# Cross-attention with layer norm on one core: the scores of two tiles in one TensorE visit

## The chip, the cores and the metric

The kernel runs on one core of one Trainium2 chip. Its time is the device time of one execution in microseconds (us), the median of several runs. The engines are TensorE (PE; its weight loads are shown apart as PEld), VectorE (DVE), ScalarE (ACT), GpSimd (POOL) and SyncE (SP), which issues most DMAs. Each engine works through its own instructions in the order in which the kernel's text names them; semaphores make one wait for another.

## The reference

Four batches of 2048 query rows (512 wide) attend to 77 context rows each, with 16 heads of 32. A mask of 77 bytes a row is non-zero where a key is left out. Behind the output projection stand a residual and a layer norm with gamma and beta.

```python
qs = (q @ wq).reshape(Bq, Lq, H, HD).transpose(0, 2, 1, 3)
ks_ = (k @ wk).reshape(Bq, Lk, H, HD).transpose(0, 2, 1, 3)
vs = (v @ wv).reshape(Bq, Lk, H, HD).transpose(0, 2, 1, 3)
scores = jnp.einsum('bhqd,bhkd->bhqk', qs, ks_) / jnp.sqrt(jnp.float32(HD))
scores = jnp.where(mask[:, None, :, :], -jnp.inf, scores)
attn = jnp.einsum('bhqk,bhkd->bhqd', jax.nn.softmax(scores, axis=-1), vs)
out = attn.transpose(0, 2, 1, 3).reshape(Bq, Lq, H * HD) @ wo + q
mu = jnp.mean(out, axis=-1, keepdims=True)
var = jnp.mean((out - mu) ** 2, axis=-1, keepdims=True)
return (out - mu) / jnp.sqrt(var + EPS) * gamma + beta
```

A row whose keys are all masked gives NaN in the reference.

## The kernel before

The 8192 query rows are 64 tiles of 128; two tiles are a pair (`u` and `u + 1`, pair number n = u / 2), four a group, sixteen a batch. The wide products (queries, output) keep full precision by splitting each operand into a high and a low part and adding three matmuls, so that a visit to the query projection (`q_visit`, L177) or the output projection (`o_proj`, L517) is 12 matmuls of 512 columns. A tile passes through these steps:

- `scores` (L309): 32 small matmuls, which the trace shows as 64. Head h = 4g + j has its 32 rows of queries and keys in row group j of the array; a tile's rows are dealt to two halves of columns. Each row group j has a PSUM bank of its own for its four heads (g = 0 to 3), 77 columns each: four banks a tile.
- `maxima` (L324), one DVE instruction a head: the score plus the mask's bias, negated, into `pbuf`, and the least of them as the exponential's bias.
- `exps` (L339), one ACT instruction a head, with the sum of its row; `recip` on DVE; `normalise` (L350), one POOL instruction a tile.
- `transp` (L373), a DVE transposition in 32x32 blocks into `B`; `regroup` (L385), twelve DMAs a pair that SP issues, put the blocks into `PT`.
- `av` (L419), 16 small matmuls a pair (32 in the trace); `av_hi` (ACT, L468) and `av_lo` (DVE, L472) empty its two banks into a high and a low part.
- `o_proj`, `residual` (DVE, L520), `moments` (DVE, L525 and L530, then four short POOL instructions, L534 to L537), `scale` (ACT, L543), `affine` (two POOL instructions, L547 and L548) and `store`.

Next to this the transposed x of a later group is loaded (`load_xT`), its high part made by ACT (`cast_xT`, L166), its low part by POOL (`split_xT`, L170), and the queries of later tiles are projected and copied from PSUM by DVE (`q_evac`, L194).

PSUM has eight banks, dealt out in a ring (`bank`): a new one waits for the readers of the one handed out eight before. `pbuf` has three buffers, the tile numbers modulo 3.

The mask of a batch is loaded in the pair of tile 10 of the batch before (`load_mask`), becomes a bias of 0 or -3.0e38 in the pair of tile 12 (`mask_bias`, L286 and L287), and `mask_min` (L291) and `mask_nan` (L295, L296) of the pair of tile 14 make a column `nz` that is EPS, or NaN where all keys of a row are masked. It is added to the variance, so that NaN comes out.

The order is written by hand: L714 to L831 is a loop over the pairs of tiles 0 to 53, and for the last ten tiles `ORDER` names each step by a letter, a tile and a part, which `do` carries out. In a pair of the loop TensorE's order is scores(u), o_proj(u-6), q_visit, av(n-2), scores(u+1), o_proj(u-5), q_visit.

Of the kernel before, what the change touches and what calls it, by code (L numbers as in the profile page):

```python
# [20 lines left out]
HD = 32  # L21
NK = 77
TAIL_K = 19
NK2 = NK + TAIL_K
NP = H // 2
PW = 160
GH = 4
NG = H // GH
# [40 lines left out]
def xattn_layernorm(  # L69
# [15 lines left out]
    nc = tc.nc  # L85
    NB = mask.shape[0]
    TPB = mask.shape[2]
# [8 lines left out]
    ring, kept, rows, summed = [], set(), {}, set()  # L96

    def bank(name):
# [25 lines left out]
    unit = ident.bitcast(F32R)  # L124
    mhalf, mneg, gates = small[:, 0:2], small[:, 2:4], small[:, 4:5]
    last_st = small[:, 8:20].rearrange("p (n s) -> p n s", n=2)
# [24 lines left out]
    def keys_of(h):  # L151
        return slice(TAIL_K, NK2) if h % 2 == 0 else slice(0, NK)
# [124 lines left out]
    def load_mask(b):  # L277
        m8 = sb.tile([P, TPB, NK], U8, tag="m8", bufs=1, name=f"m8_{b}")
        nc.sync.dma_start(m8, mask[b])
        mb = sb.tile([P, TPB, NK2], BF16, tag="mb", name=f"mb_{b}")  # L280
        nz = sb.tile([P, TPB], F32, tag="nz", name=f"nz_{b}")
        bat[b] = (mb, nz, m8)

    def mask_bias(b, ts=slice(0, TPB)):
        mb, nz, m8 = bat[b]
        nc.vector.tensor_scalar(mb[:, ts, TAIL_K:], m8[:, ts], MASKED, None, ALU.mult)  # L286
        nc.vector.tensor_scalar(mb[:, ts, :TAIL_K], m8[:, ts, NK - TAIL_K :], MASKED, None, ALU.mult)  # L287

    def mask_min(b):
        mb, nz, m8 = bat[b]  # L290
        nc.vector.tensor_reduce(nz, m8, AX.X, ALU.min)  # L291

    def mask_nan(b):
        nz = bat[b][1]
        nc.vector.tensor_scalar(nz, nz, 3.0e38, 10.0, ALU.mult, ALU.mult)  # L295
        nc.vector.tensor_scalar(nz, nz, 0.0, EPS, ALU.mult, ALU.add)  # L296


    def scores(t):
        qs = qd[t // 4]  # L300
        nmax[t] = sb.tile([P, H], F32, tag="nm", bufs=3, name=f"nm_{t}")
        sums[t] = sb.tile([P, H], F32, tag="sum", bufs=3, name=f"sum_{t}")
        sc = scs[t] = [bank(f"sc_{t}_{j}") for j in range(GH)]
        for g in range(NG):
            for half in range(0, P, P // 2):
                for j in range(GH):
                    q = slice(HD * j, HD * (j + 1))
                    r0 = (t % 4) * P + half
                    nc.tensor.matmul(  # L309
                        sc[j][half : half + P // 2, g * NK : (g + 1) * NK],  # L310
                        qs[q, g, r0 : r0 + P // 2],
                        kct[q, g, t // TPB, keys_of(j)],
                        start=True,
                        stop=True,
                    )

    def maxima(t, lo, hi):
        pb = pbuf[t % NPB]
        mb = bat[t // TPB][0]
        nm = nmax[t]  # L320
        for h in HEADS[lo:hi]:
            g, j = divmod(h, GH)
            i = slot(h)
            nc.vector.tensor_tensor_reduce(  # L324
                pb[:, i // 2, (i % 2) * NK : (i % 2 + 1) * NK],
                scs[t][j][:, g * NK : (g + 1) * NK],
                mb[:, t % TPB, keys_of(h)],
                -1.0,
                3.0e38,
                ALU.add,  # L330
                ALU.min,
                accum_out=nm[:, i : i + 1],
            )
# [53 lines left out]
    def regroup(b):  # L387
        for n in range(12):
            regroup_part(b, n, nc.sync)
# [132 lines left out]
    def moments(t):  # L522
        b, tt = divmod(t, 2)
        st = sb.tile([P, 6], F32, tag="st", bufs=3, name=f"st_{t}")
        nc.vector.bn_stats(st, od[t])  # L525
# [4 lines left out]
        nc.vector.bn_aggr(mv[:, tt, :], st)  # L530
        nz = bat[t // TPB][1]
        if tt == 1:
            k = (t - 1) % TPB
# [54 lines left out]
    def rsqrt_one(t):  # L588
        mv = mvs[t, 1]
        k = t % TPB  # L590
        eps = bat[t // TPB][1][:, k : k + 1]
        if t in summed:
            nc.gpsimd.tensor_scalar(mv[:, 2:3], mv[:, 1:2], 1.0 / D, eps, ALU.mult, ALU.add)
        else:
            nc.gpsimd.tensor_tensor(mv[:, 2:3], mv[:, 1:2], eps, ALU.add)
        nc.gpsimd.tensor_tensor(mv[:, 2:3], mv[:, 2:3], mhalf[:, :1], ALU.pow)
# [35 lines left out]
    nc.gpsimd.memset(mhalf, -0.5)  # L632
    nc.gpsimd.memset(mneg, -1.0)
    for pb in pbuf:
        nc.gpsimd.memset(pb[:, :, 2 * NK :], 0.0)
# [57 lines left out]
    for m in range(0, NG, 2):  # L693
        keys_evac(pks, m)
    mask_min(0)
    for c in range(0, NC_D, 2):
# [16 lines left out]
    evac = [(0, 0)]  # L713
    for u in range(0, 2 * CUT, 2):  # L714
        n = u // 2
# [79 lines left out]
        if u == 0:  # L795
            mask_nan(0)
            split_wv()
            recip(0)
# [37 lines left out]
        "+": residual, "u": rsqrt_one, "y": centre, "z": finish, "k": scale, "f": affine, "w": store,  # L836
        "v": bias_one, "K": stretch, "G": shift, "p": pool_scale, "I": act_mean, "J": act_squares, "M": keep,
    }
# [5 lines left out]
    def do(op, k, part=0, queue="s"):  # L844
# [8 lines left out]
        elif op in tile_parts:  # L853
            tile_parts[op](k, q4 * part, q4 * part + q4)
        elif op == "s":
# [23 lines left out]

    for word in ORDER.split():  # L880
        op, (k, part) = word[0], (word[1:] + ".").split(".")[:2]
        queue = part[-1:] if part[-1:].isalpha() else ""
        do(op, int(k), int(part[: len(part) - len(queue)] or 0), queue or "s")

# [47 lines left out]
```

## Time and profile before

| What | us |
|---|---|
| Median of three runs (514.13 to 518.13) | 514.41 |
| Profiled execution: its span, from the first to the last instruction | 510.7 |
| Median less that span | 3.7 |
| PE busy in the span | 502.1 |
| PEld busy | 387.3 |
| DVE busy | 472.1 |
| ACT busy | 471.2 |
| POOL busy | 424.3 |

The profiled execution is one other than the timed ones; of it the span is known, and the runs' time counts what lies around the span too. A row of the page's groups reads: line, engine, operation, what it writes and from what, shapes and count, then busy time and the mean of one, then idle time before it and what ended it. A row of the timeline reads: start, time to the end of the last of the rows merged into it, engine, line, operation, shapes, count. A row of stretches reads: from and to, length, then the busy time of PE, PEld, DVE, ACT and POOL with the count of instructions, the granted TensorE clock as a share of full speed, the busy share of the DMA engines, and GB/s. Times of matmuls overlap, so two starts tell more than a duration.

### The profile page before, as it was taken

What the parts mean: (1) busy time and instruction counts of PE and PEld (TensorE: products, weight loads), DVE (VectorE), ACT (ScalarE), POOL (GpSimd) and SP (SyncE); (2) the same over time, 40 slices, a digit from 0 to 9 for tenths busy, and PEclk for the clock granted to TensorE, in tenths of its full rate; (3) what the DMA queues carried; (4) which work ended last, traced back from release to release, by engine and by line L of the source; (5) the groups of instructions that cost most, each with busy time, mean ns of one, the idle gap of its engine ahead of it and who ended that gap; (6) DMA issues with size and microseconds to landing.
All of it is one profiled execution on the core that took longest, in us unless ns stands there. A gap on an engine that the chain in (4) does not pass through costs nothing.

```text
span 510.7 us, 20467 instructions
## 1 busy us (share of the span) xinstructions
PE 502.1 (98%) x6864; PEld 387.3 (76%) x6864; DVE 472.1 (92%) x2574; ACT 471.2 (92%) x2239; POOL 424.3 (83%) x382
## 2 busy tenths in 40 slices
PE   8999999999999999999999999999999999999994
PEld 6987777777777777777777777777777777777784
DVE  6798999899999888989999898889999989999997
ACT  6798999999899999999899999999899999999861
POOL 0659359988799988888989998898889989999894
PEclk9999999999999999999999999999999999999998
DMA  8946867888777888789777897788887778767665
GB/s 304 400 155 150 224 177 197 217 237 221 189 207 201 233 215 224 193 222 246 185 202 218 228 230 192 181 235 230 223 217 192 211 198 234 192 185 216 166 207 207
DMA packets 58280, 109.34 MB, mean 214 GB/s; under 512 B 9203, under 2 KB 10739, under 8 KB 58176
## 3 DMA queue, kind: packets, MB, share of 16 engines
q1 hardware_dynamic: 55776, 103.19, 73.1%
q0 software_dynamic: 1872, 4.20, 2.9%
q8 instruction: 55, 0.90, 0.8%
q10 hardware_dynamic: 528, 0.66, 0.4%
q14 instruction: 49, 0.40, 0.3%
HBM read 41.53 MB, written 16.78 MB: 114 GB/s over the span
## 4 chain that ended last, share of the span: by engine, by line
PE 87%; DVE 5%; DMA 4%; SPq 2%; POOL 1%; issue 1%; ACT 1%; DVEq 0%; POOLq 0%
PE pq L177 30%; PE po L517 29%; PE pa L419 10%; PE sc L309 10%; PE sc L517 3%; DMA PT<-B 2%; DVE B L373 2%; PE pv L243 2%; PE pk L203 1%; SPq L385 1%; DVE pbuf L324 1%; DMA stage_a<-wq 1%; PE pq L669 1%; POOL pbuf L350 0%; DVE q L194 0%
## 5 line engine op out<-in xcount | busy, mean ns | idle before, releaser
L339 ACT ACTIVATE pbuf<-pbuf,nm 128x77 f32<-128x77 f32 x1024 | 352.5, 350 | 15.0 <-DVE nm L324 13.6
L339 ACT ACTIVATION_READ_ACCUMULATOR pbuf<-pbuf,nm 128x1 f32 x1024 | 195.3, 191 | 0.0
L324 DVE CUSTOM_DVE_ANT_0 pbuf<-sc,mb 128x77 f32<-128x77 f32 x1020 | 169.9, 230 | 21.8 <-PE sc L309 21.5
L350 POOL TENSOR_TENSOR pbuf<-pbuf,ri 128x1232 f32<-128x1232 f32 x63 | 142.2, 2258 | 17.8 <-DVE ri L345 11.0
L177 PE MATMUL pq<-xth,wqh 128*128 128x512 f32 (+1 forms) x256 | 98.8, 386 | 0.0
L177 PE MATMUL pq<-xtl,wqh 128*128 128x512 f32 (+1 forms) x256 | 98.0, 383 | 0.0
L177 PE MATMUL pq<-xth,wql 128*128 128x512 f32 (+1 forms) x256 | 97.9, 383 | 0.0
L373 DVE STREAM_TRANSPOSE B<-pbuf 128x1280 f32<-128x1280 f32 x63 | 93.9, 1491 | 0.3
L517 PE MATMUL po<-woh,AH 128*128 128x512 f32 x224 | 93.3, 416 | 0.0
L517 PE MATMUL po<-wol,AH 128*128 128x512 f32 x224 | 87.7, 391 | 0.0
L517 PE MATMUL po<-woh,AL 128*128 128x512 f32 x224 | 86.7, 391 | 0.0
L324 DVE DVE_READ_ACCUMULATOR2_ANT nm<- 128x1 f32 x1024 | 83.2, 81 | 0.0
L547 POOL TENSOR_TENSOR o<-o,gam 128x512 f32<-128x512 f32 x53 | 69.9, 1319 | 14.4 <-ACT o L543 14.4
L548 POOL TENSOR_TENSOR o<-o,bet 128x512 f32<-128x512 f32 x53 | 68.4, 1290 | 4.2
L309 PEld LDWEIGHTS sc<-kct,q 32*64 32x64 f32 x4080 | 51.2, 130 | 23.7 <-issue 21.3
L170 POOL TENSOR_TENSOR xtl<-xtf,xth 128x1024 fp32r<-128x1024 f32 x28 | 67.1, 2398 | 0.0
L309 PE MATMUL sc<-kct,q 32*64 32x77 f32 x4080 | 61.2, 238 | 0.0
L419 PE MATMUL pa<-PT,vsb 96*32 96x256 f32 x960 | 58.2, 382 | 0.7 <-DMA PT<-B 0.3
L177 PEld LDWEIGHTS pq<-xth,wqh 128*128 128x128 f32 x256 | 48.1, 188 | 9.8
L177 PEld LDWEIGHTS pq<-xth,wql 128*128 128x128 f32 x256 | 48.1, 188 | 9.4
L177 PEld LDWEIGHTS pq<-xtl,wqh 128*128 128x128 f32 x256 | 48.1, 188 | 9.1
L517 PEld LDWEIGHTS po<-woh,AH 128*128 128x128 f32 x224 | 42.0, 188 | 12.0 <-DVE nm L324 0.4
(167 smaller groups left out, 707.5 us busy)
## 6 DMA issues: line engine op xcount, KB each, us to landing
PT<-B SPq DMA_DIRECT2D x355, 128.0 KB
xtf<-xT SPq DMA_DIRECT2D x28, 512.0 KB
o<-x SPq DMA_DIRECT2D x56, 256.0 KB
out<-o SPq DMA_DIRECT2D x56, 256.0 KB
PT<-B POOLq DMA_DIRECT2D x16, 128.0 KB, 5.2
o_end<-x SPq DMA_DIRECT2D x7, 256.0 KB
out<-o_end SPq DMA_DIRECT2D x7, 256.0 KB
xtf<-xT SPq DMA_DIRECT2D x4, 256.0 KB
```

Source lines behind the costliest of these rows:

```text
L170: nc.gpsimd.tensor_tensor(l, fx.pop((g, c)), h.bitcast(F32), ALU.subtract)
L177: nc.tensor.matmul(pq, w[:, c, m * P : (m + 1) * P], r[:, c, rs], start=(n == 0), stop=(n == 11))
L243: nc.tensor.matmul(pv, ctx_s[c][i][:, r, :], v[c], start=(n == 0), stop=(n == 11))
L309: nc.tensor.matmul(sc[j][half : half + P // 2, g * NK : (g + 1) * NK], qs[q, g, r0 : r0 + P // 2], kct[q, g, t // TPB, keys_of(j)], start= ...
L324: nc.vector.tensor_tensor_reduce(pb[:, i // 2, (i % 2) * NK : (i % 2 + 1) * NK], scs[t][j][:, g * NK : (g + 1) * NK], mb[:, t % TPB, keys_ ...
L339: nc.scalar.activation(p, p, AF.Exp, bias=nmax[t][:, i : i + 1], scale=-1.0, accum_out=sums[t][:, i : i + 1])
L350: nc.gpsimd.tensor_tensor(pv, pv, rv.to_broadcast((P, NP, 2, NK)), ALU.mult)
L373: nc.vector.transpose(bt.rearrange("p c q r -> p q c r"), pbuf[t % NPB].rearrange("p q (c r) -> p q c r", c=5),)
L419: nc.tensor.matmul(pas[b, g // 2][HD * j : HD * (j + 1), (g % 2) * BLK : (g % 2 + 1) * BLK], vsb[:, 2 * b // TPB, HD * h : HD * (h + 1)], ...
L517: nc.tensor.matmul(pos[t][:, cols], a[:, c, rs], w[:, c, cols], start=go, stop=done)
L547: nc.gpsimd.tensor_tensor(o, o, gam, ALU.mult)
L548: nc.gpsimd.tensor_tensor(o, o, bet, ALU.add)
```

## The change

The pairs of tiles 6 to 53 (n = 3 to 26) leave the loop. Their order is the list `PAIR`, read for each n; a letter's number is an offset to the pair's first tile (for a, b, g, i, j, P and V to n). Parts of T and e from 10 on are two heads, from 30 on (`T1.30`) one. The first three pairs stay in the loop, and `ORDER` is as before, behind three words (`JOINT`) that end what the last pair leaves.

`S` and `D` form the scores of both tiles. The eight units of row group j (two tiles of four heads) go to a bank of its own for the first six and to a shared bank for the last two; row groups 0 and 1 share one, 2 and 3 the other: six banks a pair instead of eight. `S` forms six units of each row group (the even ones begin with their shared two), `D` the rest. On TensorE a pair is now S, D, o_proj(u-6), o_proj(u-5), q_visit, q_visit, av(n-2). `av_hi` and `av_lo` come at the end of the pair or in the next.

The mask is laid out on the host with its 19 last keys ahead of the 77, so that one instruction builds the bias. `maxima` begin with a least value of 2.9e38 in place of 3.0e38: a row with all keys masked then has exponentials of 0, and its normalising gives NaN. So `nz`, `mask_min` and `mask_nan` go, and EPS is added to the variances of a pair by DVE (before: `nz` by POOL); where POOL does it for a single tile it takes a constant column, `meps`.

```diff
+CEIL = 2.9e38
+JOIN = 6
...
+PAIR = """
+q4 k-8 a-3.1 f-8 i4 x-4 S T1.30 b-3.0 L T0.1 D e0.1 b-3.1 T0.0 T1.31 T1.3 x-3 T0.3 O-6 T1.10 T0.2 e0.0 T1.11 T1.14
++-6 T1.1 e0.3 s-6 O-5 t-1 e1.15 e0.2 r0 Q5 j4 g5 Q6 n0 e1.3 e1.10 +-5 q5 B e1.14 e1.1 e1.11 k-7 V-2 s-5 w-8 t0 r1 n1
+P-1 f-7 w-7 a-2.0
+"""
+JOINT = """ a24.1 b24.0 b24.1 """
...
     def mask_bias(b, ts=slice(0, TPB)):
-        mb, nz, m8 = bat[b]
-        nc.vector.tensor_scalar(mb[:, ts, TAIL_K:], m8[:, ts], MASKED, None, ALU.mult)
-        nc.vector.tensor_scalar(mb[:, ts, :TAIL_K], m8[:, ts, NK - TAIL_K :], MASKED, None, ALU.mult)
-
-    def mask_min(b):
...
-    def mask_nan(b):
...
+        mb, m8 = bat[b]
+        nc.vector.tensor_scalar(mb[:, ts], m8[:, ts], MASKED, None, ALU.mult)
...
+    def scores_pair(b):
+        for t in (2 * b, 2 * b + 1):
...
+            scs[t] = {}
+        own = [bank(f"sc_{b}_{j}") for j in range(GH)]
+        both = [bank(f"sc_{b}_{j}") for j in ("e", "f")]
+        units = []
+        for j in range(GH):
+            mine = [(2 * b, g) for g in range(NG)] + [(2 * b + 1, g) for g in range(NG)]
+            for i, (t, g) in enumerate(mine):
+                bk, at = (own[j], i) if i < 6 else (both[j // 2], 2 * (j % 2) + i - 6)
+                scs[t][g, j] = bk[:, at * NK : (at + 1) * NK]
+            units.append(mine[6:] + mine[:6] if j % 2 == 0 else mine)
+        for i in range(6):
+            for half in range(0, P, P // 2):
+                for j in range(GH):
+                    score(*units[j][i], j, half)
+        held[b] = units
+
+    def scores_rest(b):
+        units = held.pop(b)
+        for i in (6, 7):
+            for js in ((0, 2), (3, 1)):
+                for half in range(0, P, P // 2):
+                    for j in js:
+                        score(*units[j][i], j, half)
...
-                3.0e38,
+                CEIL,
...
-            nc.gpsimd.tensor_tensor(rn[:, 0, :], mv[:, :, 1], nz[:, k : k + 2], ALU.add)
+            nc.vector.tensor_scalar(rn[:, 0, :], mv[:, :, 1], EPS, None, ALU.add)
...
-    for u in range(0, 2 * CUT, 2):
+    for u in range(0, JOIN, 2):
...
-        if k == TPB - 2 and m + 1 < NB:
-            mask_min(m + 1)
-            mask_nan(m + 1)
...
+            lo, size = (q4 * part, q4) if part < 10 else (2 * part - 20, 2) if part < 20 else (part - 20, 1)
+            tile_parts[op](k, lo, lo + size)
...
+    for n in range(JOIN // 2, CUT):
+        pair(n)
+    for word in (JOINT + ORDER).split():
+        do(*read(word))
```

`pair(n)` reads `PAIR` word by word: S and D call the two functions above, L and B load and build the next batch's mask in the pairs of tiles 10 and 12 of a batch, and the other words go to `do` with the offset added. Words that would repeat what the loop's last pair did are left out.

More of the change, by code (lines that the diff above doesn't have):

```diff
@@ L124, in xattn_layernorm @@
     unit = ident.bitcast(F32R)
-    mhalf, mneg, gates = small[:, 0:2], small[:, 2:4], small[:, 4:5]
+    mhalf, mneg, gates, meps = small[:, 0:2], small[:, 2:4], small[:, 4:5], small[:, 5:6]
     last_st = small[:, 8:20].rearrange("p (n s) -> p n s", n=2)
@@ L306, in scores, with score @@
                 for j in range(GH):
[L307 to L315, printed above, removed]
+                    score(t, g, j, half)
+    def score(t, g, j, half):
+        q = slice(HD * j, HD * (j + 1))
+        r0 = (t % 4) * P + half
+        return nc.tensor.matmul(
+            scs[t][g, j][half : half + P // 2],
+            qd[t // 4][q, g, r0 : r0 + P // 2],
+            kct[q, g, t // TPB, keys_of(j)],
+            start=True,
+            stop=True,
+        )
+    def scores_pair(b):
+        for t in (2 * b, 2 * b + 1):
+            nmax[t] = sb.tile([P, H], F32, tag="nm", bufs=3, name=f"nm_{t}")
+            sums[t] = sb.tile([P, H], F32, tag="sum", bufs=3, name=f"sum_{t}")
+            scs[t] = {}
[20 more added lines that the diff above has]
+                        score(*units[j][i], j, half)
     def maxima(t, lo, hi):
@@ L633, in xattn_layernorm @@
     nc.gpsimd.memset(mneg, -1.0)
+    nc.gpsimd.memset(meps, EPS)
     for pb in pbuf:
@@ L795, in xattn_layernorm @@
         if u == 0:
-            mask_nan(0)
             split_wv()
@@ L836, in xattn_layernorm @@
         "+": residual, "u": rsqrt_one, "y": centre, "z": finish, "k": scale, "f": affine, "w": store,
-        "v": bias_one, "K": stretch, "G": shift, "p": pool_scale, "I": act_mean, "J": act_squares, "M": keep,
+        "v": bias_one, "L": load_mask, "B": mask_bias, "K": stretch, "G": shift, "p": pool_scale, "I": act_mean, "J": act_squares, "M": keep,
     }
@@ L878, in do, with read, pair @@
             (av_hi if op == "c" else av_lo)(k // 2, k % 2, True)
-    for word in ORDER.split():
+    def read(word):
         op, (k, part) = word[0], (word[1:] + ".").split(".")[:2]
         queue = part[-1:] if part[-1:].isalpha() else ""
-        do(op, int(k), int(part[: len(part) - len(queue)] or 0), queue or "s")
+        return op, int(k or 0), int(part[: len(part) - len(queue)] or 0), queue or "s"
+    def pair(n):
+        u = 2 * n
+        for word in PAIR.split():
+            op, k, part, queue = read(word)
+            if op == "S":
+                scores_pair(n)
+            elif op == "D":
+                scores_rest(n)
+            elif op in "LB":
+                m, at = divmod(u, TPB)
+                if at == TPB - (6 if op == "L" else 4) and m + 1 < NB:
+                    do(op, m + 1)
+            elif op == "P" and "." not in word:
+                regroup(n + k)
+            elif op in "Qq":
+                if op == "Q" or divmod(2 * n + k, 4) in qp:
+                    do(op, 2 * n + k)
+            elif op in "gij":
+                do(op, n + k)
+            elif op in "PVab":
+                if op in "PV" or n + k > JOIN // 2 - 3:
+                    do(op, n + k, part, queue)
+            elif u + k >= 0:
+                do(op, u + k, part, queue)
+    for n in range(JOIN // 2, CUT):
+        pair(n)
+    for word in (JOINT + ORDER).split():
+        do(*read(word))
 def kernel(
@@ L904 @@
     B, S, Dm = x.shape
-    NKc = c.shape[1]
     N = B * S
@@ L914 @@
         ),
-        "mask": np.ascontiguousarray(mk.reshape(B, S // P, P, NKc).transpose(0, 2, 1, 3)),
+        "mask": np.ascontiguousarray(
+            np.concatenate([mk[..., NK - TAIL_K :], mk], -1).reshape(B, S // P, P, NK2).transpose(0, 2, 1, 3)
+        ),
         "wq": np.ascontiguousarray(L0_xattn_wq),
```

27 lines of the change are left out of this document (8 added, 19 removed).

## The prediction

> **What bounds the kernel now.** I read the page's busy shares first, then the chain of work that ended last, then the row of stretches for the 24 pairs that the change rewrites, and last the timeline of one pair.
>
> ```profile
> span 510.7 us, 20467 instructions
> PE 502.1 (98%) x6864; PEld 387.3 (76%) x6864; DVE 472.1 (92%) x2574; ACT 471.2 (92%) x2239; POOL 424.3 (83%) x382
> ...
> PE 87%; DVE 5%; DMA 4%; SPq 2%; POOL 1%; issue 1%; ACT 1%; DVEq 0%; POOLq 0%
> ...
> 59.73:419.07 359.34, 359.34 (x4993) 273.46 (x4992) 336.89 (x1898) 347.65 (x1671) 310.57 (x256) 1.00 0.80 212
> ...
> 216.02:230.97 14.95, 14.95 (x210) 11.39 (x209) 13.42 (x79) 14.52 (x71) 13.21 (x12) 1.00 0.84 225
> ```
>
> TensorE carries 87% of the chain. The stretch from the first score matmul of tile 6 (59.73) to that of tile 54 (419.07) holds exactly the 24 pairs that become new. Its columns are length, then busy time of PE, PEld, DVE, ACT and POOL. TensorE is busy in all of it: 359.34 / 24 = **14.97 us a pair**, at full granted clock (1.00). Behind it stand ACT with 347.65 / 24 = 14.49, DVE with 336.89 / 24 = 14.04 and POOL with 12.94. The second stretch is one pair without mask work; there DVE needs only 13.42. So whatever TensorE gains beyond 14.97 - 14.49 = 0.48 us a pair is stopped by ACT, whose instructions the change does not reduce.
>
> What a pair costs on TensorE beside streaming is seen at a score visit, and how fast the visit runs, in the timeline cut off at ever later moments (count of matmuls, and time to the end of the last of them) and in the durations of the line (least, median, most):
>
> ```profile
> 208.94 0.39 PE L177 MATMUL pq<-xtl,wqh 128*128 128x512 f32 x1
> 209.17 0.39 PE L177 MATMUL pq<-xth,wql 128*128 128x512 f32 x1
> 209.49 0.95 PE L309 MATMUL sc<-kct,q 32*64 32x77 f32 x64
> 210.37 0.50 PE L517 MATMUL po<-woh,AH 128*128 128x512 f32 x1
> 210.71 0.39 PE L517 MATMUL po<-wol,AH 128*128 128x512 f32 x1
> 210.94 0.39 PE L517 MATMUL po<-woh,AL 128*128 128x512 f32 x1
> ```
> ```profile
> 209.49 0.32 PE L309 MATMUL sc<-kct,q 32*64 32x77 f32 x8
> ...
> 209.49 0.52 PE L309 MATMUL sc<-kct,q 32*64 32x77 f32 x32
> ...
> 210.08 0.36 PE L309 MATMUL sc<-kct,q 32*64 32x77 f32 x14
> ...
> L309 PE MATMUL sc<-kct,q x128: 224/226/277, 203.0 to 210.2; 32*64 32x77 f32 x128
> ```
>
> Wide matmuls start 0.23 apart (208.94 to 209.17). Into the small ones it takes 0.32, and the first wide one behind them takes 0.34 until the next: a visit costs 0.09 + 0.11 = **0.20 us of switching**. The visit itself lasts 0.88. Its first 32 matmuls end after 0.52 and all 64 after 0.95. One matmul lasts 0.226, so the first half starts one every (0.52 - 0.226) / 31 = 9.5 ns (from the 8th to the 32nd end 0.20 / 24 = 8.3 ns), the last fourteen one every (0.36 - 0.226) / 13 = 10.3 ns, while the second half as a whole takes 0.43 / 32 = 13.4 ns each, with a pause in it. The rest of the 0.88, about 0.27, is the fill, the pause and the drain, paid once a visit.
>
> **The change part by part.**
>
> *One visit instead of two (24 pairs).* The work is the same 128 matmuls, directly behind the attention visit, so one switch of 0.20 goes. The second 64 matmuls cost 64 x 9.5 = 0.61 if they only stream, 0.86 if they run like the second half of a visit; at best 64 x 8.3 = 0.53. I take 0.61, since the starts behind the pause, the last fourteen, are near it. TensorE then needs 14.97 - 0.20 - (0.88 - 0.61) = **14.50 us a pair** (14.42 to 14.77). That is ACT's 14.49. Neither works without a wait, so I take 14.52: 0.45 x 24 = **-10.8 us** (-4.8 to -13.2).
>
> *Waits that this adds.* The shared banks get their second row group's scores only in D. D may not write a bank while DVE reads it, so it waits for T1.30, one head. T1.30 starts about when 16 to 32 matmuls are through, 0.4 to 0.5 after the visit's start, and lasts 0.24; D's first matmul is due after 48 x 2 = 96 matmuls, at about 0.9. It costs nothing (0 to 0.2). Behind D on TensorE stand the output and query projections. The visit itself waits for q4, which empties the bank of the last query visit, and DVE waits in turn for the visit:
>
> ```profile
> 203.89 0.24 DVE L324 CUSTOM_DVE_ANT_0 pbuf<-sc,mb 128x77 f32<-128x77 f32 x1 [1.40 <-PE sc L309]
> 204.06 0.08 DVE L324 DVE_READ_ACCUMULATOR2_ANT nm<- 128x1 f32 x1
> ...
> 204.23 0.36 ACT L339 ACTIVATE pbuf<-pbuf,nm 128x77 f32<-128x77 f32 x1 [0.34 <-DVE nm L324]
> ...
> 208.23 1.50 DVE L373 STREAM_TRANSPOSE B<-pbuf 128x1280 f32<-128x1280 f32 x1
> 209.66 0.65 DVE L525 BATCH_NORM_STATS2 st<-o 128x6 f32<-128x512 f32 x1
> 210.34 0.18 DVE L530 BATCH_NORM_AGGREGATE mv<-st 128x2 f32<-128x6 f32 x1
> ```
>
> Today DVE sits idle 1.40 at 203.89. A hand-over costs about 0.1 (the first exponential starts 0.34 after the first minimum, which lasts 0.24). The new loop on DVE is 13.42 of work, 0.1 to the visit, 0.5 to T1.30 and the small addition of EPS, 0.1: **14.1 us**, under 14.52. So DVE hides, with 0.4 to spare.
>
> *The mask.* It is built in one instruction; `mask_min` and `mask_nan` go. They lie on DVE under TensorE's full row, so what goes is worth nothing. Where the new one stands matters. The two rows of today's build, one of `mask_nan`, and GpSimd beside them:
>
> ```profile
> 112.70 1.58 POOL L547 TENSOR_TENSOR o<-o,gam 128x512 f32<-128x512 f32 x1 [0.81 <-ACT o L543]
> ...
> 112.36 0.78 DVE L286 TENSOR_SCALAR mb<-m 128x1232 bf16<-128x1232 uint8 x1
> 113.06 1.40 DVE L287 TENSOR_SCALAR mb<-m 128x304 bf16<-128x304 uint8 x1
> 114.37 0.24 DVE L345 RECIPROCAL ri<-sum 128x16 f32<-128x16 f32 x1
> ...
> 248.91 1.29 POOL L548 TENSOR_TENSOR o<-o,bet 128x512 f32<-128x512 f32 x1
> ...
> 248.94 1.29 DVE L295 TENSOR_SCALAR nz<-nz 128x16 f32<-128x16 f32 x1
> ...
> L295 DVE TENSOR_SCALAR nz<-nz x1: 162/162/162, 29.1 to 29.1; 128x16 f32<-128x16 f32 x1
> ```
>
> 1232 elements take 0.70 before GpSimd is at work; the next 304 take 1.40 and end with GpSimd's instruction (112.70 + 1.58 = 114.28). Sixteen elements take 1.29 beside GpSimd, over the same 1.29 as its addition, and 0.16 alone. A `tensor_scalar` of DVE from SBUF to SBUF thus waits until GpSimd's running instruction is done. In the new order the mask (B) stands three instructions behind r0, and r0 releases GpSimd's normalise, 2.26 us:
>
> ```profile
> 204.92 2.26 POOL L350 TENSOR_TENSOR pbuf<-pbuf,ri 128x1232 f32<-128x1232 f32 x1
> ...
> 199.37 2.40 POOL L170 TENSOR_TENSOR xtl<-xtf,xth 128x1024 fp32r<-128x1024 f32 x1
> 202.31 1.27 POOL L547 TENSOR_TENSOR o<-o,gam 128x512 f32<-128x512 f32 x1 [0.55 <-ACT o L543]
> 203.67 1.29 POOL L548 TENSOR_TENSOR o<-o,bet 128x512 f32<-128x512 f32 x1
> ...
> 207.63 0.68 DVE L520 TENSOR_TENSOR o<-po,o 128x512 f32<-128x512 f32 x1
> ```
>
> B is reached a residual (0.60 to the transpose's start) and a query copy (0.58) later, 1.3 with hand-overs, so it waits about 1.0, then runs 1536 / 1232 x 0.70 = 0.87. Behind it on DVE stand s-5, t0, r1 and q4, for which TensorE waits. 1.9 less the 0.4 to spare is 1.5 us in each of three pairs: **+4.5 us** (0.4 each without the wait, 1.9 each without slack: 1.2 to 5.7).
>
> *EPS as a DVE addition, 24 times.* The same kind of instruction, 128x2, with 0.1 between its start and the next at best. It comes 1.3 + 0.8 (statistics and aggregate) = 2.1 after r0, so it can wait 0.3 for the normalise; t0 behind it needs that same normalise, so nothing is added.
>
> *Moves.* av moves to the pair's end and its high and low parts into the next pair; O-6 needs the last low part at its ninth product, some 2 us after D, and DVE has it before. Loads, stores and the twelve regrouping DMAs keep their number on SP; av uses tiles regrouped a pair before. All cost nothing under TensorE's row. At the end two low parts (0.6 each) stand ahead of tile 54's first minimum: **+0.5** (0 to 1.2). The first stretch and `ORDER` stay as they are.
>
> *Sum.* -10.8 + 4.5 + 0.5 = -5.8: a span of 510.7 - 5.8 = 504.9. The runs' median of 514.41 lies 3.7 above the profiled span, for what is around it, which I keep: **508.6 us**.
>
> **The rivals.**
>
> 1. *The visit runs dry.* The second 64 matmuls go like a second half, 0.86, and only the switch is saved: 14.77 a pair, -4.8 + 4.5 + 0.5 = +0.2, **514.6**. For it speak the pause and the 13.4 ns; against it the 10.3 ns behind the pause. [...]
> 2. *GpSimd's ring decides.* r1, n1, two scale-and-shift pairs, one split, n0, t0 and r1 again follow one another: 0.24 + 2.26 + 2 x 2.61 + 2.40 + 2.26 + 1.43 and three hand-overs = 14.1 (a scale-and-shift pair is 204.92 - 202.31 = 2.61, t0 209.66 - 208.23). From 0.9 of stretch it passes 14.97 and all engines follow it. L547 ran 1.58 instead of 1.27 where DVE's mask lay in front of it; should the four scales and shifts each lose 0.3, the ring is 15.3: (15.3 - 14.97) x 24 + 4.5 + 0.5 = +12.9, **527**. Against it: POOL has 14.97 - 12.94 = 2.0 us free in a pair, and the one new DVE instruction of this kind stands where the normalise runs.
> 3. *The mask hides and ACT alone bounds.* 14.49 a pair, -11.5, masks +1.2: **504.1**. For it: GpSimd may start the normalise late; against it: B's place behind r0.
>
> **How the numbers follow.** Forecast 0.43 (own range 504 to 513), visit dry 0.20, ring 0.19, hidden mask 0.18. A measurement of this kernel tells about 1%, 5.1 us, from no change. Of the forecast some 0.31 lies below 509.3; with the hidden mask that is 0.49 faster. The ring gives 0.18 slower; 0.33 is within. The bounds sum to -12.0 at the low end (-13.2 + 1.2) and +2.1 at the high (-4.8 + 5.7 + 1.2); with 0.4 of scatter below and half of the ring's way above the range is 502 to 520. The rest of the ring, 0.15, is left out.
>
> **What would show it.** One block of 128 score matmuls after each attention block, about 1.5 us to the first output matmul; pairs of 14.5 us; ACT busy in nearly all of a pair; in the pairs of tiles 12, 28 and 44 a DVE mask instruction of about 1.9 us and a TensorE gap of 1.5 before the next scores. A block of 1.75 shows rival 1, a normalise or split well over its length rival 2, mask pairs as long as the others rival 3. The prediction is wrong if a wait for q4, T1.30 or the regrouped tiles stands ahead of the visits in every pair.

## The result and the profile after

The changed kernel takes **520.53 us** (median of four runs, 520.04 to 521.77) beside 514.27 (511.69 to 518.13) for the kernel before: a ratio of **1.0135, 95% interval 1.010 to 1.017**. It is slower, and outside the range of 502 to 520. The page of the changed kernel, beside the rows of before:

```profile
span 518.8 us, 20291 instructions
PE 498.5 (96%) x6864; PEld 391.3 (75%) x6864; DVE 469.7 (91%) x2581; ACT 471.3 (91%) x2239; POOL 420.1 (81%) x359
q8 instruction: 54, 0.88, 0.8%
PE 79%; DVE 8%; DMA 5%; ACT 3%; issue 2%; SPq 2%; DVEq 0%; ACTq 0%
```

TensorE is busy for 3.6 us less (498.5 for 502.1), yet the span is 8.1 longer, and TensorE's share of the chain falls from 87% to 79%. The row `q8` (packets, MB, share of the DMA engines) has its part to play below. By stretches (from and to, length, busy time of PE, PEld, DVE, ACT, POOL, granted clock, DMA share, GB/s), first the 24 new pairs, then six of them without a disturbance, then the tail; the last fence is the tail before.

```profile
59.89:425.82 365.93, 355.78 (x4993) 277.44 (x4992) 336.20 (x1912) 347.45 (x1671) 306.21 (x235) 1.00 0.77 208
154.53:242.65 88.12, 88.12 (x1253) 68.95 (x1250) 82.69 (x473) 86.27 (x414) 76.93 (x58) 1.00 0.80 217
425.82:518.80 92.98, 84.67 (x1188) 66.31 (x1184) 86.15 (x424) 75.30 (x360) 80.68 (x92) 0.99 0.69 197
```
```profile
419.07:510.70 91.63, 84.45 (x1185) 66.25 (x1184) 85.97 (x426) 75.00 (x362) 80.64 (x95) 0.98 0.68 198
```

An undisturbed new pair takes 88.12 / 6 = **14.69 us**, 0.28 less than the 14.97 of before: 24 of them should have saved 6.8. Instead the 24 pairs take 365.93 in place of 359.34. So 6.6 + 6.8 = **13.4 us** were lost in single places. The chain of waits on TensorE (waited for: us in total, times, longest) names them:

```profile
PE sc_e L310 <- issue: 2.8, 2, 1.7
PE sc L310 <- issue: 2.8, 2, 1.7
PE sc_f L310 <- DVE nm L353: 2.6, 1, 2.6
PE sc L310 <- DVE q L203: 2.4, 2, 1.2
PE po L546 <- issue: 0.6, 1, 0.6
```

The kernel before has none of these rows. Three things stand here: one wait for DVE's first minimum (D, the rest of the scores, behind T1.30, one head's minimum), two for q4, DVE's copy of the last query visit out of its bank, and five stalls that end with "issue", where TensorE waited for nothing that a semaphore shows. A row of waits counts from the end of the matmul before; from here on a gap is counted from the start of one matmul to the start of the next, which makes it about 0.2 longer where a score matmul stands before it.

**The first new pair.** DVE in the timeline of pair 3 (start, length, line, operation):

```profile
60.72 1.51 DVE L402 STREAM_TRANSPOSE B<-pbuf 128x1280 f32<-128x1280 f32 x1
62.95 0.25 DVE L374 RECIPROCAL ri<-sum 128x16 f32<-128x16 f32 x1 [0.73 <-ACT pbuf L368]
63.12 0.63 DVE L203 COPY q<-pq 128x512 f32<-128x512 f32 x1
63.66 0.22 DVE L353 CUSTOM_DVE_ANT_0 pbuf<-sc_f,mb 128x77 f32<-128x77 f32 x1
```

T1.30, the last row, stands behind what the old loop left on DVE for tile 5: its last minima (up to the transposition's start at 60.72), transposition, reciprocal, copy. The reciprocal waits 0.73 for ACT's last exponential of that tile besides. TensorE stood from 61.17 to 63.95, 2.78.

**The mask.** POOL and DVE in pair 6 and the start of pair 7:

```profile
118.24 2.26 POOL L379 TENSOR_TENSOR pbuf<-pbuf,ri 128x1232 f32<-128x1232 f32 x1 [0.93 <-DVE ri L374]
...
118.63 0.68 DVE L203 COPY q<-pq 128x512 f32<-128x512 f32 x1
119.22 2.09 DVE L294 TENSOR_SCALAR mb<-m 128x1536 bf16<-128x1536 uint8 x1
121.24 0.68 DVE L554 BATCH_NORM_STATS2 st<-o 128x6 f32<-128x512 f32 x1
...
124.14 0.63 DVE L203 COPY q<-pq 128x512 f32<-128x512 f32 x1
```

The mask took 2.09; it ends 0.8 after POOL's normalise (118.24 + 2.26 = 120.50). q4 comes at 124.14 behind it, and TensorE's next visit, which needs the bank that q4 empties, stood for 1.42 (123.40 to 124.82). Pair 15 lost 1.43 in the same way; in pair 23 nothing is seen, because pair 22 had already lost 1.93.

**Stalls without a wait.** In pairs 5, 8, 22 and 25 and once in the tail. Pair 25 on TensorE:

```profile
394.45 0.23 PE L310 MATMUL sc_f<-kct,q 32*64 32x77 f32 x1
396.36 0.34 PE L310 MATMUL sc_e<-kct,q 32*64 32x77 f32 x2 [1.69 <-issue]
396.63 0.50 PE L546 MATMUL po<-woh,AH 128*128 128x512 f32 x1
...
398.13 0.63 PE L546 MATMUL po<-wol,AH 128*128 128x512 f32 x1
398.56 0.63 PE L546 MATMUL po<-woh,AL 128*128 128x512 f32 x1
```

Two score matmuls short of the visit's end TensorE stands for 1.91. The wide matmuls behind it start 0.43 apart (398.13 to 398.56) in place of 0.23; the clock is the reason, and in the second row of stretches it reads 0.64 (over 397.11 to 400.52 alone it is 0.50):

```profile
393.00:396.00 3.00, 1.68 (x130) 1.52 (x126) 2.39 (x17) 3.00 (x10) 2.92 (x3) 1.00 0.52 119
396.00:400.00 4.00, 3.64 (x11) 2.82 (x12) 3.33 (x43) 4.00 (x25) 3.92 (x4) 0.64 0.77 197
```

That costs pair 25 another 1.6 (18.22 - 14.69 - 1.91).

What ends these stalls shows when the instructions are counted. `q8` brought 0.88 MB in 54 packets, 16.3 KB each. TensorE executed 6864 matmuls, as many loads and 237 semaphore and drain instructions, 13,965 / 54 = 259 a packet. For every gap of TensorE over 0.6 us behind 50 us, counted in the trace:

```
start   gap   instructions executed before   of these mod 256   after a packet's end
 61.17  2.78    1616    80    wait for DVE (D)
 93.62  1.38    2497   193    1.30
123.40  1.42    3169    97    wait for DVE (q4)
140.65  1.15    3777   193    1.32
243.14  1.43    6545   145    wait for DVE (q4)
348.34  1.93    9665   193    1.39
394.45  1.91   10945   193    1.47
464.20  1.30   12993   193    1.45
```

The five gaps without a wait all begin at the same place of the count, 5, 23, 5 and 8 times 256 instructions apart, and end 1.3 to 1.5 us after a packet has come in. With the 259 a packet of the whole run that puts a packet at 256 instructions. The reading that fits is that TensorE had executed one packet of instructions and the next was not there; the experiments put it to the test. The ledger: +0.2 (start) - 6.8 (pairs) + 2.8 (pair 3) + 2.85 (mask) + 6.1 (stalls in pairs: 1.38, 0.92, 1.93 and 1.91; the 1.15 of pair 8 lies between two wide matmuls, 0.23 apart by themselves) + 1.6 (clock) + 1.35 (tail, 92.98 - 91.63) = **8.1**, as the spans.

### The profile page after: what moved, and what is told of

The parts are those of the page before. It is cut to its first block, busy times and chain, and to the rows that moved or that the text cites. A ratio compares the mean times of both kernels' runs of the same rounds, so it can differ in the third digit from the quotient of the medians.

```text
span 518.8 us, 20291 instructions
## 1 busy us (share of the span) xinstructions
PE 498.5 (96%) x6864; PEld 391.3 (75%) x6864; DVE 469.7 (91%) x2581; ACT 471.3 (91%) x2239; POOL 420.1 (81%) x359
## 4 chain that ended last, share of the span: by engine, by line
PE 79%; DVE 8%; DMA 5%; ACT 3%; issue 2%; SPq 2%; DVEq 0%; ACTq 0%
PE pq L186 27%; PE po L546 26%; PE pa L448 8%; PE sc L310 6%; PE sc L546 3%; DVE B L402 3%; DMA PT<-B 2%; ACT pbuf L368 2%; DVE pbuf L353 2%; SPq L414 2%; PE pv L252 2%; PE sc_e L310 2%; PE pk L212 1%; DMA out<-o 1%; PE pq L695 1%
## 5 line engine op out<-in xcount | busy, mean ns | idle before, releaser
L353 DVE CUSTOM_DVE_ANT_0 pbuf<-sc,mb 128x77 f32<-128x77 f32 x828 | 143.5, 233 | 6.4 <-PE sc L310 6.0
L546 PE MATMUL po<-woh,AH 128*128 128x512 f32 x224 | 91.1, 407 | 0.0
L353 DVE DVE_READ_ACCUMULATOR2_ANT nm<- 128x1 f32 x1024 | 84.5, 82 | 0.0
L574 POOL TENSOR_TENSOR o<-o,gam 128x512 f32<-128x512 f32 x53 | 68.8, 1299 | 1.0 <-ACT o L570 1.0
L310 PE MATMUL sc<-kct,q 32*64 32x77 f32 x3312 | 56.6, 238 | 5.2 <-issue 2.8
L310 PEld LDWEIGHTS sc<-kct,q 32*64 32x64 f32 x3312 | 49.5, 130 | 11.3 <-issue 6.8
L546 PEld LDWEIGHTS po<-woh,AH 128*128 128x128 f32 x224 | 42.4, 189 | 10.8 <-DVE ri L374 0.4
```

Source lines behind the costliest of these rows:

```text
L310: return nc.tensor.matmul(scs[t][g, j][half : half + P // 2], qd[t // 4][q, g, r0 : r0 + P // 2], kct[q, g, t // TPB, keys_of(j)], start=True,
L353: nc.vector.tensor_tensor_reduce(pb[:, i // 2, (i % 2) * NK : (i % 2 + 1) * NK], scs[t][g, j], mb[:, t % TPB, keys_of(h)], -1.0, CEIL, ALU ...
L546: nc.tensor.matmul(pos[t][:, cols], a[:, c, rs], w[:, c, cols], start=go, stop=done)
L574: nc.gpsimd.tensor_tensor(o, o, gam, ALU.mult)
```

## The experiments

Two theories were held against each other. **Late instructions**: the visit of 128 small matmuls with their loads is 256 instructions in 1.7 us, faster than packets come. **The order**: the mask and the waits in the new order, wherever the packets lie.

**The new mask in the old order.** `mask_bias` in one instruction, CEIL, no `mask_min` and `mask_nan`, EPS by DVE; loop and visits as before.

```diff
-        nc.vector.tensor_scalar(mb[:, ts, TAIL_K:], m8[:, ts], MASKED, None, ALU.mult)
-        nc.vector.tensor_scalar(mb[:, ts, :TAIL_K], m8[:, ts, NK - TAIL_K :], MASKED, None, ALU.mult)
+        nc.vector.tensor_scalar(mb[:, ts], m8[:, ts], MASKED, None, ALU.mult)
```

> The kernel before with the mask's part of the change alone: bias built in one instruction at its old place, running minimum from 2.9e38, EPS added by DVE, nz gone; the order, the two score visits and the banks as before. Theory (the loss comes from the new order alone): TensorE's row stays full, 14.97 us a pair, 0 +- 2 us. Rival (the new mask itself costs, by DVE's addition in 24 pairs and by the one instruction waiting for GpSimd): 2.8 us or more slower, with gaps before the scores of the pairs behind the builds.

Measured: 513.04 beside 513.48, ratio 0.9986 (0.9952 to 1.0021). The mask's new form alone costs nothing; what is lost comes with the order. Its trace, of the slowest of its ten executions (517.41), holds two stalls without a wait, so the old order can have them too:

```profile
PE sc L299 <- issue: 1.1, 1, 1.1
PE po L507 <- issue: 1.1, 1, 1.1
```

**Moving the packets.** 16, 32 or 48 extra score matmuls of 8 columns in the first new pair, into columns that nobody reads; each is four TensorE instructions, so all later packets end 64, 128 or 192 instructions earlier in the work.

```diff
         held[b] = units
+        if b == JOIN // 2:
+            for i in range(SHIFT):
...
+                nc.tensor.matmul(own[j][half : half + P // 2, 500:508], ..., kct[q, 0, 0, :8], start=True, stop=True)
```

> The changed kernel with 16 more small matmuls (32 matmuls and 32 weight loads in the trace, so 64 TensorE instructions) of 8 columns into unused columns of the score banks, placed where the first new pair waits 2.8 us anyway; everything behind is moved by a quarter of a 256-instruction packet. Theory (four visits stand still 0.9 to 1.9 us because TensorE's instructions, brought by DMA in 16 KB packets, come late): the stalls move to other pairs than 5, 8, 22 and 25, their sum changes by 2 us or more. Rival (a wait for DVE or ACT in those pairs): the same pairs stall by the same amounts, time within 1 us of the changed kernel.

> The same with 32 more small matmuls, 128 instructions, half a packet. Theory (late instructions): again other pairs stall, and the sum of the stalls differs from that of the changed kernel (6.1 us) and of the quarter shift. Rival (a wait for DVE or ACT): the same pairs, the same sum, time within 1 us.

> The same with 48 more small matmuls, 192 instructions, three quarters of a packet. Theory (late instructions): other pairs stall; of the four shifts (0, 64, 128, 192) the best and the worst lie 2 us or more apart. Rival (a wait for DVE or ACT): the same pairs, the same sum, time within 1 us.

Measured: ratios 1.0086 (1.0053 to 1.0118), 1.0107 (1.0036 to 1.0178) and 1.010 (1.0034 to 1.0167); medians 518.0, 519.2 and 518.8. The times hardly tell the shifts apart, the traces do, and there the rival (the same pairs stall) fails. The stalls of pairs 5, 8, 22 and 25 are gone in all three; others stand in pairs 6 and 17 (64), in pairs 3 and 15 (128), in pairs 3, 7 and 10 (192), again all at 193 of 256. The gaps for the mask stay in pairs 7, 15 and 23, except that with 64 the stall of pair 6 hides that of pair 7. With 128 pair 3 lost 3.90: T1.30 was done at 63.76, but TensorE went on only at 66.35. Each shift exchanged one set of unlucky pairs for another.

**The mask in four parts.** Loaded in the pair of tile 6, built in four parts in the pairs of tiles 8 to 14, each ahead of r0, the reciprocal that releases POOL's normalise.

```diff
-e0.2 r0 Q5 ... q5 B e1.14
+e0.2 B r0 Q5 ... q5 e1.14
+                if op == "B" and at in (8, 10, 12, 14) and m + 1 < NB:
+                    mask_bias(m + 1, slice(2 * at - 16, 2 * at - 12))
```

> The changed kernel with the next batch's mask loaded in the pair of tile 6 and its bias built in four instructions of four tiles each, one in each of the pairs of tiles 8, 10, 12 and 14, directly ahead of r0, where GpSimd waits for r0. Theory (the build waits for the normalise that r0 has released and runs 2.1 us in one piece ahead of q4): the gaps of 1.4 us before the scores of pairs 7, 15 and 23 go, the four parts cost 0.2 to 0.4 us each on DVE, hidden by its slack: -2.5 to -4.3 us against the changed kernel, less or more by the stalls of late instructions that move with it. Rival (those gaps are not the mask's): they stay at +0.49 us of the same visits.

Measured: ratio 1.0125 (1.0084 to 1.0165). In the trace no visit waits for q4 any more, and pairs 7, 15 and 23 have visits of 1.77, 1.75 and 1.69. So the gap belonged to the mask and its place. Of the stalls those of pairs 5, 22 and 25 are still there (0.85, 1.93 and 1.34), pair 8 is 0.3 longer than an undisturbed one, the tail has one of 1.91, and the time does not show what the mask gave:

```profile
PE sc L310 <- issue: 3.4, 2, 1.7
PE sc_f L310 <- DVE nm L353: 2.5, 1, 2.5
PE sc_e L310 <- issue: 1.7, 2, 1.1
```

**The hand-over.** The first new pair makes its first query visit (Q5) ahead of its scores, so that DVE has time to end tile 5.

```diff
+        if n == JOIN // 2:
+            words.remove("Q5")
+            words.insert(words.index("S"), "Q5")
```

> The changed kernel with the first query visit of the first new pair (n = 3) ahead of its scores instead of behind its output projections; all else as it was. Theory (D of that pair waits for T1.30, which stands on DVE behind the last old tile's minima, transposition and sums): the wait of 2.8 us within visit 3 falls below 0.5, the time by 2 to 2.8 us. Rival (DVE and ACT are behind there and TensorE only waits at another place): the wait shows up in pair 3 or 4 at another instruction and the time changes by less than 1 us.

Measured: ratio 1.011 (1.0077 to 1.0142). The wait of 2.78 is gone (a visit of 1.78), but pair 4 now waits 1.50 for q4: net 1.3, between what theory and rival said. The mask's gaps of pairs 7 and 15 stay.

**Half the instructions.** Score matmuls over all 128 rows of a tile: a visit has 64 matmuls and 64 loads in the trace instead of 128 and 128. The second kernel is the kernel before with the same edit.

```diff
-            for half in range(0, P, P // 2):
-                for j in range(GH):
-                    score(*units[j][i], j, half)
+            for j in range(GH):
+                score(*units[j][i], j)
```

> The changed kernel with each score matmul over the whole 128 rows of a tile instead of two halves of 64: half the score instructions (128 instead of 256 matmuls and loads a pair), the same results, banks and order. Theory (a visit of 256 instructions outruns their delivery): no visit stands still without a wait, the sum of those stalls falls from 6.1 us to under 1; the visit itself may come out at 1.2 to 1.9 us, as two column halves no longer run side by side. Rival (the stalls are waits for other engines): they stay. Time 508 to 515 us by the theory, 517 to 523 by the rival.

> The kernel before with score matmuls over whole tiles in both visits of a pair, nothing else. It tells what the wider matmul does by itself: if it makes a visit of 0.88 us longer or shorter, twice a pair. Theory (small visits of 128 instructions never outran the delivery): no stall goes, the time moves only by the visit's own length, within 3 us of before. Rival (the kernel before lost time to late instructions too): faster by 3 us or more.

Measured: 1.0252 (1.0183 to 1.0321) and 1.0215 (1.0152 to 1.0278). Both are slower than either side expected (524.34 and 523.84 us). In the changed order every undisturbed visit takes 1.95 and every such pair 14.93, so the wide form costs what the new order saves; in the old one a visit takes 1.06 in place of 0.88 and a pair 15.29. So in the wide form the new order saves 0.36 a pair, 8.6 in all, and gives it back in the 2.58 of pair 3, the mask's three gaps of 1.4, and a halved clock behind two of these gaps (0.50 behind that of pair 15). TensorE's waits in the changed order with whole tiles:

```profile
PE sc L309 <- DVE q L203: 3.0, 3, 1.0
PE sc_f L309 <- DVE nm L350: 2.3, 1, 2.3
PE pq L692 <- ACT xth L153: 1.0, 1, 1.0
PE pw L661 <- POOL ident L653: 0.9, 1, 0.9
```

No row with "issue" is left, while pair 3 and the mask wait as before: two theories, two causes, both real. The first goes with the number of instructions in a visit and the pace at which they are used up, which the wide form changes together; the second belongs to the order.

**Whole tiles for the last four of eight units** (with the two edits above; `HALVED = 4`, 192 instructions a visit).

> The changed kernel with the spread mask and the moved query visit, and with the last four of a visit's eight units in matmuls over the whole tile, the first four in halves: 96 matmuls and 96 loads a visit instead of 128 and 128. Theory (the delivery of instructions falls behind in the later part of a long visit, where a whole-tile unit at 0.028 x 8 = 0.22 us costs no more than a halved one at 0.013 x 16 = 0.21): visits of 1.7 to 1.8 us, stalls without a wait under 2 us in sum, 24 x (14.97 - 14.72) = 6 us gained, the wait of 1.5 us in pair 4 left: 509 to 513 us, at or under before. Rival (waits for other engines take the gain): 515 us or more.

Measured: ratio 1.0069 (1.0045 to 1.0094). No stall in the pairs, but the visit takes 1.97 and a pair 14.94: the estimate for the mixed visit was wrong, and the time, 516.59, is the rival's.

**Mask in parts and hand-over together**, then the same with 128 and 192 instructions of shift.

> The same without the wider matmuls: the changed kernel with the spread mask and the moved query visit alone. Theory: the gaps of the mask go (three of 1.4), the hand-over gains 1.3, the stalls of late instructions stay at 4 to 8 us: 513 to 518 us, 2 us or more above the run with wider matmuls. Rival (late instructions are not what is left): the two runs lie within 1 us.

> e10's kernel (spread mask, Q5 of the first new pair ahead of its scores) with the 32 extra score matmuls (128 TensorE instructions, about 0.8 us) of the run with 128 shifted instructions, so that the instruction packets lie against the visits as they did there. Theory (what is left of the loss are late instructions, whose place the count of instructions sets): the stalls without a wait in pairs 5, 22 and 25 (1.91, 1.48 and 1.17 in e10) are gone, at most one of 0.7 to 1.4 stands anywhere in the 24 pairs, pair 4 still waits 1.5, and the time is 511 to 514, a ratio of 0.993 to 0.999 to the kernel before. Rival (the stalls come with the order itself, wherever the packets lie): three or more stalls without a wait are left, and the time is 515 to 518, a ratio of 1.002 to 1.007.

> The same with 48 extra score matmuls (192 TensorE instructions, about 1.2 us), as in the run with 192 shifted instructions, where stalls without a wait stood in pairs 7 and 10. Theory (late instructions, whose place the count of instructions sets): stalls without a wait in pairs 7 and 10, of 1.2 to 1.5 each, and none in pairs 5, 22 and 25; pair 4 waits 1.5; 512 to 515, a ratio of 0.995 to 1.001. Rival (the order itself): stalls in pairs 5, 22 and 25 as in e10, 515 to 518, a ratio of 1.002 to 1.007.

Measured: 1.0035 (1.0006 to 1.0063); 0.9981 (0.9959 to 1.0003); 0.9978 (0.996 to 0.9996). The first lies 0.8 under the run with whole tiles, not 2 above it: the wider visits cost as much as the stalls did, so this comparison says little of the stalls. The first has stalls in pairs 5, 8, 22 and 25 (1.91, 0.77, 1.48, 1.17), the second in 3, 15 and 18 (1.25, 1.17, 1.33), the third in 3, 10 and 13 (1.49, 1.40, 1.07). Of the places expected, pair 10 came true and pair 7 did not, and three stalls stood in each where at most one and just two were expected (three or more is what the rival of the second run had said). They stand in other pairs than without a shift, and the times are the theory's (511.37 and 511.71). Pair 4 waited 0.65, not 1.5, since pair 3 was late.

**Which packets stall.** In all seventeen traces (both kernels and these fifteen) most ends of packets cost nothing, even within a visit. What sets the others apart is how fast the packet was executed. In all of them, behind 40 us, by the time in which TensorE executed a packet's 256 instructions (waits for another engine left out):

```
executed in        packets   a gap of 0.2 us or more behind it   of 0.6 or more
up to 2.2 us          36                  35                           32
over 2.2 us          788                   -                           12
```

The one packet in the first row without a gap has 0.23 behind it, the usual distance of two wide matmuls. In the kernel before, the quickest packet took 5.1; in the changed kernel four took 1.6 to 2.2, each within one visit, and in the pairs just those four stalled. Such a packet ends some 235 to 260 instructions after the visit's first (later in the four visits of pair 3 that extra matmuls make longer). This can be steered: with one more 8-column matmul (four instructions) in each pair the end moves by only 2 in three pairs instead of 14, and stays where it is put.

```diff
         held[b] = units
+        pad(own[0], b)
...
+    def pad(bk, b):
+        q = slice(0, HD)
+        nc.tensor.matmul(bk[: P // 2, 500:508], qd[b // 2][q, 0, : P // 2], kct[q, 0, 0, :8], start=True, stop=True)
...
     pw = bank("pw")
+    for i in range(12):
+        nc.tensor.matmul(pw[:, :8], warm[:, :P], warm[:, :8], start=True, stop=True)
```

The first kernel has the upper part alone, the second the warm-up matmuls of 24 instructions too.

> The changed kernel with one extra 8-column score matmul (four TensorE instructions, about 0.03 us) at the end of the first part of each visit. A packet holds 256 instructions; with four more in each pair its end moves by only 2 instructions in three pairs instead of 14. In every third pair (5, 8, 11, 14, 17, 20, 23, 26) it then falls 236 to 250 instructions into the visit, in the others at 65 to 80 and 145 to 165. Theory (TensorE stalls where a packet begins and ends within one visit, since its 256 instructions are then executed in under 2.2 us and the next packet is not there): stalls without a wait of 0.8 to 1.9 us in six to eight of these eight pairs and in no other, about 10 us in all instead of 6, so 522 to 527, a ratio of 1.017 to 1.027. Rival (stalls by chance, or by the time of the packet's transfer alone): two to five stalls, in any pairs, 518 to 522, a ratio of 1.010 to 1.017.

> The same kernel with twelve extra 8-column warm-up matmuls (24 instructions) at the very start, where TensorE waits for its first data. The ends of the packets fall 24 instructions earlier in each visit: at 212 to 226, 40 to 56 and 120 to 140. Theory (a packet within one visit): no stall without a wait in any of the 24 pairs, while the mask's gaps in pairs 7, 15 and 23 (1.4 each or hidden) and pair 3's wait of 2.8 stay; 511 to 515, a ratio of 0.995 to 1.002, so that 6 to 8 us of the changed kernel's 520.5 are late packets alone. Rival (chance, or the transfer's time): two to five stalls, 517 to 522, a ratio of 1.008 to 1.017, as without the 24.

Measured: **1.0202** (1.0114 to 1.029) and **1.002** (0.9987 to 1.0054). Without the 24 there are stalls of 1.68, 1.40, 1.36, 2.13, 1.45, 1.32 and 1.19 in pairs 5, 8, 11, 14, 17, 20 and 26, and the mask's wait covers the one in pair 23; with them there is none, and the mask's gap shows in all three pairs (1.42, 1.42, 1.40). TensorE's waits in the first and in the second:

```profile
PE sc L310 <- issue: 5.7, 4, 1.9
PE sc_f L310 <- DVE nm L358: 2.5, 1, 2.5
PE sc L310 <- DVE q L203: 2.4, 2, 1.2
PE sc_f L310 <- issue: 2.3, 2, 1.2
PE sc_e L310 <- issue: 1.0, 1, 1.0
```
```profile
PE sc L310 <- DVE q L203: 3.6, 3, 1.2
PE sc_f L310 <- DVE nm L358: 2.2, 1, 2.2
```

The profiled spans are 520.3 and 510.9: nine microseconds lie between two kernels that differ by 24 instructions in the warm-up. With the packets placed well the change is about as fast as the kernel before: what made it slower is late instructions, while the mask and pair 3 eat what the pairs gain.

**All together**: mask in parts, hand-over, extra matmul and 24 instructions.

> As the run before this, with the mask in four parts and Q5 of the first new pair ahead of its scores (e10's kernel with the extra matmul a pair and the 24 instructions). Theory: no stall without a wait in the 24 pairs, no gap for the mask, pair 4's wait of 1.5 is what is left; 508 to 512, a ratio of 0.990 to 0.998. Rival: two to five stalls, 513 to 518, a ratio of 1.000 to 1.008, as e10.

Measured: **507.86** (507.46 to 508.26), ratio **0.9881** (0.9818 to 0.9943), faster than both. Its page, its waits on TensorE and the stretch of its 24 new pairs:

```profile
span 505.7 us, 20420 instructions
```
```profile
PE sc L310 <- DVE q L203: 1.3, 1, 1.3
```
```profile
62.19:414.14 351.95, 350.62 (x5029) 274.22 (x5029) 333.09 (x1908) 344.23 (x1655) 306.46 (x235) 1.00 0.80 215
```

Of all the waits above pair 4's 1.3 is left. The 24 pairs take 351.95, 7.4 less than before, of which 2.5 are given back ahead of them by the projection that moved (they begin at 62.19 instead of 59.73).

## Why the prediction was wrong

The sign and the size were wrong: a span of 504.9 was forecast, 518.8 came, 13.9 more. Step by step:

- *One visit instead of two*: "I take 0.61" for the second 64 matmuls. The visit takes 1.69, as three rows of pair 13 show:

```profile
213.24 0.28 PE L310 MATMUL sc_e<-kct,q 32*64 32x77 f32 x1
...
214.93 0.50 PE L546 MATMUL po<-woh,AH 128*128 128x512 f32 x1
215.26 0.39 PE L546 MATMUL po<-wol,AH 128*128 128x512 f32 x1
```

  The second half thus costs 1.69 - 0.88 = 0.81, near rival 1's 0.86: only the switch and a little more are saved. This term was mis-sized by 4.0 (-6.8 for -10.8). Its low end of -13.2, 14.42 a pair, was also below the ACT bound of 14.49 that the prediction itself had set. (Rival 3's 504.1, which does keep to that bound, leaves out the end's +0.5.) ACT did not bound: 86.27 / 6 = 14.38 a pair under 14.69.
- *Waits that this adds*: for T1.30 "it costs nothing (0 to 0.2)". True of a pair that follows a new one; in the first, where DVE still holds the old loop's work, 2.8. The steady pair was walked, the joint at its start was not.
- *The mask*: 1.5 in each of three pairs forecast, 1.42 and 1.43 measured, the third hidden by a stall (in e14 all three are there). Place, cause and size were right: 2.85 for 4.5.
- *EPS* and the *moves* cost nothing, as said; GpSimd's ring (rival 2) did not decide.
- *The end*: +0.5 forecast, 1.35 measured, most of it the stall at 464.20.
- *What stood nowhere in the sum*: "The work is the same 128 matmuls". It is, but they are 256 instructions in a row, as many as a packet. 6.1 of stalls and 1.6 of clock were missed, and no rival had them. The page of before shows the row of instruction packets (`q8`, 55 packets, 0.90 MB), but how fast one is used up was no part of the prediction.
- *The offset*: 3.7 was kept between span and runs. The same execution's time less its span is 520.62 - 518.8 = 1.8, and so it is in nearly every run. The other 1.9 of the 3.7 is the difference between the profiled execution of before (510.7 + 1.8 = 512.5) and the median of three others; the later medians of that kernel, 512.23 to 513.48, lie nearer to the 512.5. That put the forecast 1.9 too high.

In sum, with the mask's 2.85 for 4.5 and the start's 0.2: 4.0 + 2.8 - 1.65 + 6.1 + 1.6 + 0.85 + 0.2 = 13.9; less 1.9 that is the 12.0 between 508.6 and the 520.6 of the profiled execution.

## What to carry to other kernels

Count TensorE's instructions between places where it is slow: in these traces a run of small matmuls that used up one packet of 256 (matmuls and loads) in up to 2.2 us left TensorE standing, mostly for 1 to 2 us, wherever a packet started and ended within it (35 of 36 such packets had a gap of 0.2 us or more behind them, 32 one of 0.6), though each of its instructions is cheap. Such gaps show by their place: the changed kernel's five that ended with "issue" all came at 193 modulo 256. Where a packet's end moves by only 2 in three pairs, 24 idle instructions in the warm-up took all seven away (a span of 510.9 for 520.3). Where a new order takes over from an old one, walk the first repetition with what the old one left on every queue, not only the steady one.

## What the runs showed of the hardware

TensorE's clock fell after some short gaps. In pair 25 one gap of 1.91 was followed by 3.41 us at half the clock (0.50 from 397.11 to 400.52); in pair 22 a gap of 1.93 left it at full:

```profile
347.00:350.30 3.30, 1.60 (x124) 1.44 (x124) 2.71 (x20) 3.30 (x12) 3.22 (x3) 1.00 0.79 173
350.30:354.30 4.00, 4.00 (x25) 3.29 (x26) 3.61 (x39) 3.87 (x23) 3.92 (x4) 1.00 0.75 215
```

The mask's gap of 1.26 in pair 15 of the kernel with whole tiles (246.38 to 247.64) was enough; the stretches around the fall there:

```profile
246.41:249.83 3.42, 2.43 (x55) 2.11 (x50) 3.14 (x15) 2.82 (x6) 2.79 (x3) 1.00 0.69 158
249.83:253.24 3.41, 3.41 (x10) 2.63 (x9) 3.41 (x44) 3.41 (x21) 3.31 (x3) 0.50 0.35 97
```

The pace agrees with a half (wide matmuls 0.43 apart for 0.23). The changes come in steps of 3.41 us: in the changed kernel's trace they lie 115, 116 and 150 such steps after the clock first became full (at 4.58), in that of the kernel before 147 (after 4.47), and with whole tiles the half clock lasted one step, 249.83 to 253.24. The gap of pair 25 lay whole in one step (393.70 to 397.11), that of pair 22 was divided between two at 349.32. That alone does not tell them apart: with the mask in four parts a gap of 1.93 in pair 22, with 1.83 of it in one step, left the clock at full. What decides it stays open.

In pair 13 of the changed kernel the 9th to the 25th small score matmul of the visit start 8.3 ns apart, the last 96 of the 128 on average 12.7, and the wider form over 128 rows takes 1.95 for the visit though it has half as many. Why the pace falls was not tried. Open is also what sends for a packet: the time from one's arrival to TensorE's next start was 1.2 to 1.5 in all 44 stalls of 0.6 us or more, but twelve of them came behind packets that were executed in more than 2.2 us, five of them at one place of the tail.
